# The first 60 microseconds of a fused attention and feed-forward block: early loads, products of zeros, and projections pulled in one at a time

## The chip, the core and the metric

The kernel runs on one core of one Trainium2 chip. The metric is the device time of one execution in microseconds (us). Engines: TensorE (PE; its weight loads are PEld), VectorE (DVE), ScalarE (ACT), GpSimd (POOL) and SyncE (SP). SP and POOL issue the transfers.

## The reference

A pre-norm layer on x of 2 x 1024 x 512 (float32), cut to what matters here:

```python
x = x + attention(layernorm(x), w_q, w_k, w_v, w_o)   # 32 heads of 16
x = x + ffn(layernorm(x), w_gate, w_up, w_down)       # ternary weights, quantised tokens, I = 1376
# attention: softmax(q k^T / sqrt(16)) v, all 1024 keys for each query
```

## The kernel before

**Tiling.** The heads are taken in four groups `g` of eight, and each group in two steps `s` of four heads; the queries of a batch `b` in two halves `h` of 512. That gives 32 steps `(b, h, g, s)`, in the order batch, half, group, step. A step has eight tiles `i` of 128 keys. Queries and keys are used as a high and a low part (`hi`, `lo`), each a tile of type fp32r.

**The main loop** runs over turns `T`. In a turn, `scores` makes the products of one key tile `i` of one step for the exponentials (`exp_mm`, `pse`, L558, then ACT's exp, L562) and the products for the row maxima of the next step (`max_mm`, `psm`, L518, then DVE's `max_reduce`, L528); `weigh_values` (`pso`, L588) multiplies exponentials with values. Maxima of step n are made in turns 8n to 8n + 7; the exponentials begin ten turns after (`LE = 10`), so in turns 0 to 9 there are only maxima. `max_rows` (`psn`, L541, copied to `mrow`) turns a step's maxima into a row.

**Fillers.** Between these products a planner (class `Fillers`) puts pieces of other work, written as generators: projections of keys, queries and values (`project_qk`, `psk` and `psq`, L419; `project_v`, `psv`, L459), normalisation and transposes of tokens (`norm_inputs`: statistics L353, centring L362, transposes `psx` L370, copies `xnT` L371), later the output projection and the feed-forward part. A filler says `take` when it needs a PSUM tile, `give` when it is done with it, `gap` to sleep for some turns and `pe` for what TensorE time it used. Each turn grants a budget: `pace` spreads the remaining work over the remaining turns, between 960 and 1800 ns a turn. Everything is emitted in this order; each engine works its own instructions in order.

**Round trips.** Projected keys, queries and values go to device memory (`kD`, L444; `qD`, L441; `vD`, L473 on POOL's queue) and come back rearranged: `load_k` (`kst`, L492), `load_q` (`qst`, two tiles, L500), `load_v` (L506). `lo` is made by DVE (L428) where the filler is `fast`; otherwise ACT copies (L431) and POOL makes `hi` and `lo` (L432, L433). All other transfers of the start are on SP's queue: tokens (L348), projection weights (`proj_weights`, L401).

**The start.** By hand: four tiles of tokens, weights of keys and queries of group 0; normalise the first half, project its keys and queries, load them back, normalise the second half (whose tokens use the same four buffers), project its keys, load the rest and step 1. Then the loop. Five turns before a step begins its keys and queries must exist:

```python
if (T + 5) % NT == 0 and 1 < (T + 5) // NT < NSTEP:      # NT = 8
    n = (T + 5) // NT
    b, h, g, s = steps[n]
    fill.ensure(f"k_{b}_{g}_0", f"k_{b}_{g}_1", f"q_{b}_{g}_{h}")
```

`ensure` runs the planner with an unlimited budget (`self.run(1e9)`) until the named fillers are done, so every other filler that is ready runs along. In turn 11 it asks for group 1 (step 2): after turn 10's products TensorE's order has the second half of `psv` of group 1 for the first tokens, `psk` of group 1 for the second half, `psv` of group 1 for the second half, and `psk` of group 2.

**Sums of the feed-forward weights** (`weight_sums`: POOL's transfers L680, ACT L696) start when the values of group 0 are projected; their quantisation (POOL L733, DVE L735) follows.

Of the kernel before, what the change touches and what calls it, by code (L numbers as in the profile page):

```python
# [30 lines left out]
class Fillers:  # L31
# [43 lines left out]
    def _step(self, task):  # L75

        task["begun"] = True
        if task["take"]:
            task["take"] = False
            task["kind"] = self.kind = self._bank()  # L80
            self.held.append((task["kind"], None))
        try:
            what = next(task["gen"])
        except StopIteration:
            self.tasks[task["list"]].remove(task)
            self.done.add(task["name"])
            return 0.0
        if what[0] == "pe":
            task["cost"] = max(task["cost"] - what[1], 0.0)
            return what[1]  # L90
        if what[0] == "gap":
            task["wake"] = self.now + what[1]
        elif what[0] == "take":
            task["take"] = True
            task["short"] = len(what) > 1
        else:
            task["short"] = False
            self.held.remove((task["kind"], None))
            self.held.append((task["kind"], self.now + 1))
        return 0.0  # L100

    def _candidates(self):
# [49 lines left out]
    def ensure(self, *names):  # L152

        start = self.now
        while not set(names) <= self.done:
            self.run(1e9)
            assert self.now - start < 400, names


# [57 lines left out]
def kernel(  # L217
# [39 lines left out]
    SCALE = 0.25  # L257
    LEAD = 2

    const = ctx.enter_context(tc.tile_pool(name="const", bufs=1))  # L260
    sb = ctx.enter_context(tc.tile_pool(name="sb", bufs=1))
    sp = ctx.enter_context(tc.tile_pool(name="sp", bufs=3))
# [79 lines left out]
    def norm_inputs(b, half, fast, need=()):  # L342

        tiles = range(4 * half, 4 * half + 4)
        xs = {}
        for t in tiles:
            xs[t] = sb.tile([P, H], F32, tag="x", name=f"x_{b}_{t}", bufs=4)
            nc.sync.dma_start(xs[t], x[b, t * P : (t + 1) * P, :])  # L348
        yield ("gap", 4)
        mv = sp.tile([P, 4, 2], F32, tag="mv1", name=f"mv1_{b}_{half}")  # L350
        for i, t in enumerate(tiles):
            st = sp.tile([P, 6], F32, tag="bn", name=f"bn1_{b}_{t}")
            nc.vector.bn_stats(st, xs[t])  # L353
# [7 lines left out]
        for i, t in enumerate(tiles):  # L361
            nc.vector.tensor_scalar(  # L362
                xs[t], xs[t], mv[:, i, 0:1], r[:, i : i + 1], ALU.subtract, ALU.mult
            )
            if not fast:
                yield ("gap", 1)
            yield ("take",)
            ps = spare(f"psx_{b}_{t}")
            for c in range(KC):
                nc.tensor.transpose(ps[:, c * P : (c + 1) * P], xs[t][:, c * P : (c + 1) * P], ident)  # L370
            nc.scalar.copy(  # L371
                xnT[b, half][:, :, i * P : (i + 1) * P], ps.rearrange("p (c t) -> p c t", c=KC)
            )
            yield ("give",)
            yield ("pe", 700.0)
# [20 lines left out]
        while not set(names) <= fill.done:  # L396
            yield ("gap", 1)

    def proj_weights(ap, g, name):
        w = sb.tile([P, KC, P], F32, tag="w", name=name, bufs=4)  # L400
        nc.sync.dma_start(  # L401
            w, ap.rearrange("(c p) e -> p c e", p=P)[:, :, g * P : (g + 1) * P]
        )
        return w

    def project_qk(b, g, which, h, have, fast=False):
        if which == 1 and h == 1:
            w = wt.pop((b, g))
        else:
            w = proj_weights((wqT, wkT)[which], g, f"w{'qk'[which]}_{b}_{g}_{h}")  # L410
            if which == 1:
                wt[b, g] = w
            yield ("gap", 4)
        yield from done(have)
        yield ("take",)
        name = f"{'qk'[which]}_{b}_{g}_{h}"
        ps = spare(f"ps{name}")
        for c in range(KC):
            nc.tensor.matmul(  # L419
                ps, w[:, c, :], xnT[b, h][:, c, :], start=(c == 0), stop=(c == KC - 1)  # L420
            )
            if c < KC - 1:
                yield ("pe", 860.0)
        hi = sb.tile([P, QB], F32R, tag="hi", name=f"hi_{name}", bufs=2)
        lo = sb.tile([P, QB], F32R, tag="lo", name=f"lo_{name}", bufs=2)
        if fast:
            nc.scalar.copy(hi, ps)
            nc.vector.tensor_tensor(lo, ps, hi.bitcast(F32), ALU.subtract)  # L428
        else:
            full = sb.tile([P, QB], F32, tag="full", name=f"full_{name}", bufs=1)  # L430
            nc.scalar.copy(full, ps)  # L431
            nc.gpsimd.tensor_copy(hi, full)  # L432
            nc.gpsimd.tensor_tensor(lo, full, hi.bitcast(F32), ALU.subtract)  # L433
        yield ("give",)
        yield ("pe", 860.0)
        yield ("gap", 3)
        for l, part in enumerate((hi, lo)):
            if which == 0:
                dst = qD[b, g, h][l].rearrange("(e a d) q -> a e d q", a=2, d=16)
                for a in range(2):  # L440
                    nc.sync.dma_start(dst[a], part.bitcast(F32))  # L441
            else:
                dst = kD[b, g].rearrange("(e l d) q -> l e d q", l=2, d=16)[l]
                nc.sync.dma_start(dst[:, :, h * QB : (h + 1) * QB], part.bitcast(F32))  # L444
            yield ("gap", 1)

    def step_k(n):
        b, _, g, s = steps[n]
        return kD[b, g].rearrange("(r s e) q -> s r e q", r=4, s=2)[s]

    def project_v(b, g, half, have):
        w = proj_weights(wvT, g, f"wv_{b}_{g}_{half}")
        yield ("gap", 4)
        yield from done(have)
        yield ("take",)
        ps = spare(f"psv_{b}_{g}_{half}")
# [28 lines left out]
    kst, qst, vt = {}, {}, {}  # L485
    pm, mrow, probs = {}, {}, {}

    def load_k(n, halves=((0, S),)):
        if halves[0][0] == 0:
            kst[n] = sb.tile([P, S], F32R, tag="kst", name=f"kst_{n}", bufs=3)  # L490
        for first, end in halves:
            nc.sync.dma_start(kst[n][:, first:end].bitcast(F32), step_k(n)[:, :, first:end])  # L492

    def load_q(n):
        b, h, g, s = steps[n]
# [672 lines left out]
    def now(gen):  # L1168
        for _ in gen:
            pass  # L1170
# [1 line left out]

    firsts = [norm_inputs(0, half, True) for half in range(2)]
    next(firsts[0])
    keys = [project_qk(0, 0, 1, half, [], True) for half in range(2)]
    queries = project_qk(0, 0, 0, 0, [], True)
    next(keys[0])
    next(queries)
    next(firsts[1])
    early = [project_v(0, 0, half, [f"ln_0_{half}"]) for half in range(2)]  # L1180
    next(early[0])
    for k, ap in enumerate((s_gate, s_up, s_down)):
        t = const.tile([P, 1], F32, name=f"scale{k}")
        nc.sync.dma_start(t, ap.partition_broadcast(P))
        s_sb.append(t)
    next(early[1])
    fill.kind = "s"
    now(firsts[0])
    now(keys[0])
    now(queries)  # L1190
    load_k(0, ((0, QB),))
    load_q(0)
    now(firsts[1])
    now(keys[1])
    load_k(0, ((QB, S),))
    load_k(1)
    load_q(1)
    fill.kind = "o"
    fill.done |= {"ln_0_0", "ln_0_1", "k_0_0_0", "k_0_0_1", "q_0_0_0"}

    def due_k(n):

        return NT * n - 5

    def due_v(n):
        return NT * n + 8
# [2 lines left out]
    for n, (b, h, g, s) in enumerate(steps):  # L1209
        if s == 0:  # L1210
            first_step[b, h, g] = n

    for half in range(2):
        fill.add(f"v_0_0_{half}", early[half], due=due_v(0), cost=3760.0)

    for b in range(B):
        if b:
# [11 lines left out]
        for g in range(NG):  # L1229
            n = first_step[b, 0, g]  # L1230
            if b or g:
                fill.add(f"k_{b}_{g}_0", project_qk(b, g, 1, 0, have[:1]), due=due_k(n), cost=3440.0)
                fill.add(f"k_{b}_{g}_1", project_qk(b, g, 1, 1, have), [f"k_{b}_{g}_0"], due=due_k(n), cost=3440.0)
                fill.add(f"q_{b}_{g}_0", project_qk(b, g, 0, 0, have[:1]), due=due_k(n), cost=3440.0)
                for half in range(2):
                    fill.add(f"v_{b}_{g}_{half}", project_v(b, g, half, [have[half]]), due=due_v(n), cost=3760.0)
# [45 lines left out]
    for T in range(LE + NT * NSTEP + 1):  # L1282
# [4 lines left out]

        fill.scores = int(T < LE - 1 or T >= NT * NSTEP)

        if (T + 5) % NT == 0 and 1 < (T + 5) // NT < NSTEP:  # L1290
            n = (T + 5) // NT
# [87 lines left out]
```

## Time and profile before

| | us |
|---|---|
| median of 3 runs | 1255.51 (1252.96 to 1260.84) |
| profiled execution | 1261.95, of which the span is 1259.9 |
| PE busy | 1174.2 (93%) |
| DVE busy | 854.6 (68%) |
| ACT busy | 690.2 (55%) |
| POOL busy | 251.4 (20%) |
| transfers | 136.88 MB, mean 109 GB/s |

The profiled execution is one more execution than the runs of the median, and its own time is its span and 2.05 us around it. A share of busy time is a mean over the whole span; the stages differ, so the stage tables (busy time by engine between two points of the span, with the clock granted to TensorE as a share of its full one) say more.

### The profile page before, as it was taken

Reading aid. Unit: us, or ns where it says so; the run is one execution under the profiler, and the core shown is the slowest. Engines: PE = TensorE matmul, PEld = TensorE weight load, DVE = VectorE, ACT = ScalarE, POOL = GpSimd, SP = SyncE. Lnnn points to the kernel's source line nnn. Section 1 sums busy time; section 2 is a strip of 40 time slices with the busy share of each in tenths; the row PEclk is TensorE's granted clock in tenths of the full one; section 3 lists DMA queues with packets and bytes.
Section 4 is the critical chain, followed back from the end, with each engine's and each line's share of the span. In section 5 each row is a group of like instructions: output and inputs, shape, how many; then the busy total and the mean of one; then the engine's idle time right before and its main releaser. Section 6 shows DMA issues by size and latency. Waiting matters only on the chain.

```text
span 1259.9 us, 21791 instructions
## 1 busy us (share of the span) xinstructions
PE 1174.2 (93%) x8898; PEld 526.7 (42%) x8898; DVE 854.6 (68%) x1181; ACT 690.2 (55%) x873; POOL 251.4 (20%) x286
## 2 busy tenths in 40 slices
PE   4657999999899999999999999999999998999996
PEld 2424443544345444444444444534444433344343
DVE  5431659788766667778876665576887678877173
ACT  1113855566455555666655555556666555566654
POOL 0122335556310100222001001112201011121020
PEclk9877999999999999999999999999999999999998
DMA  4446674656531432232323624233335233242200
GB/s 139 127 128 198 189 262 130 205 136 200 186 121 62 130 114 74 80 92 71 95 70 96 130 96 142 89 102 112 87 63 87 69 104 64 67 75 49 63 9 33
DMA packets 97887, 136.88 MB, mean 109 GB/s; under 512 B 33572, under 2 KB 54052, under 8 KB 97788
## 3 DMA queue, kind: packets, MB, share of 16 engines
q1 hardware_dynamic: 89916, 110.20, 30.6%
q0 software_dynamic: 7872, 25.30, 6.3%
q8 instruction: 69, 1.13, 0.4%
q14 instruction: 30, 0.25, 0.1%
HBM read 91.34 MB, written 38.24 MB: 103 GB/s over the span
## 4 chain that ended last, share of the span: by engine, by line
PE 75%; DVE 11%; issue 6%; DMA 4%; ACT 2%; POOL 1%; SPq 1%; POOLq 0%; DVEq 0%; ACTq 0%
PE pse L558 23%; PE pso L588 17%; PE psm L518 8%; PE psq L419 4%; PE psk L419 4%; DVE pm L528 4%; PE psv L459 4%; PE psy L770 4%; PE py L917 2%; PE pu L851 2%; PE pg L851 2%; PE psn L541 1%; DMA x<-in_x 1%; DMA qD<-hi_q 1%; PE psx L370 1%
## 5 line engine op out<-in xcount | busy, mean ns | idle before, releaser
L528 DVE TENSOR_REDUCE pm<-psm 128x2 f32<-128x1024 f32 x512 | 621.5, 1221 | 304.9 <-PE pse L558 192.7
L562 ACT ACTIVATE e<-pse 128x1024 f32<-128x1024 f32 x512 | 522.7, 1023 | 423.3 <-PE pse L558 316.8
L518 PE MATMUL psm<-kst,qst 32*128 32x512 f32 x2048 | 370.1, 445 | 8.0 <-ACT e L562 4.6
L558 PE MATMUL pse<-qst,kst 32*128 32x512 f32 x2048 | 370.5, 444 | 6.2 <-DVE pm L528 5.3
L558 PEld LDWEIGHTS pse<-qst,kst 32*128 32x128 f32 x2048 | 150.5, 184 | 344.3 <-issue 193.2
L588 PE MATMUL pso<-e,v 128*32 128x512 f32 x2048 | 274.5, 606 | 0.5 <-ACT po L597 0.4
L558 PE MATMUL pse<-mrow,onesr 2*128 2x512 f32 x1024 | 205.1, 398 | 0.0
L518 PEld LDWEIGHTS psm<-kst,qst 32*128 32x128 f32 x2048 | 151.0, 184 | 25.6 <-ACT e L562 13.0
L419 PE MATMUL psk<-xnT,wk 128*128 128x512 f32 x128 | 78.7, 733 | 23.3 <-DMA wk<-in_wkT 16.1
L558 PEld LDWEIGHTS pse<-mrow,onesr 2*128 2x128 f32 x1024 | 95.0, 184 | 3.4 <-ACT mrow L545 0.2
L865 POOL TENSOR_TENSOR g<-g 128x460 f32<-128x460 f32 (+1 forms) x36 | 34.2, 950 | 274.0 <-ACT g L861 274.0
L588 PEld LDWEIGHTS pso<-e,v 128*32 128x32 f32 x2048 | 40.5, 108 | 96.4 <-issue 93.5
L459 PE MATMUL psv<-wv,xnT 128*128 128x128 f32 x512 | 70.8, 289 | 2.8 <-ACT full_q L431 2.0
L459 PEld LDWEIGHTS psv<-wv,xnT 128*128 128x128 f32 x512 | 62.5, 197 | 17.3 <-issue 12.7
L419 PE MATMUL psq<-xnT,wq 128*128 128x512 f32 x128 | 66.5, 626 | 0.0
L473 POOL DMA_DIRECT2D vD<-vst x32 | 18.0, 565 | 210.6 <-ACT vst L471 210.6
L733 POOL TENSOR_SCALAR low<-raws,whalf 128x512 bf16<-128x512 f32 (+2 forms) x35 | 52.8, 1509 | 21.0 <-DVE wd L735 7.0
L770 PE MATMUL psy<-wo,OT 128*128 128x512 f32 x96 | 51.0, 639 | 2.3 <-DVE inter L873 1.8
L419 PEld LDWEIGHTS psk<-xnT,wk 128*128 128x128 f32 x128 | 25.5, 227 | 54.2 <-issue 45.4
L432 POOL CAST hi_q<-full_q 128x512 fp32r<-128x512 f32 x15 | 9.3, 619 | 152.6 <-ACT full_q L431 149.4
L851 PEld LDWEIGHTS <-xqT 128*128 128x128 bf16 x288 | 22.4, 98 | 37.6 <-issue 23.3
L826 POOL TENSOR_SCALAR xn<-x,mv,a 128x512 f32<-128x512 f32 x12 | 25.1, 2090 | 56.7 <-DVE a L803 56.6
(209 smaller groups left out, 872.3 us busy)
## 6 DMA issues: line engine op xcount, KB each, us to landing
qst<-qD SPq DMA_DIRECT2D x64, 256.0 KB
v<-vD SPq DMA_DIRECT2D x32, 512.0 KB
kst<-kD SPq DMA_DIRECT2D x31, 512.0 KB
qD<-hi_q SPq DMA_DIRECT2D x32, 256.0 KB
qD<-lo_q SPq DMA_DIRECT2D x32, 256.0 KB
vD<-vst POOLq DMA_DIRECT2D x32, 256.0 KB, 5.6
x<-in_x SPq DMA_DIRECT2D x20, 256.0 KB
wq<-in_wqT SPq DMA_DIRECT2D x16, 256.0 KB
```

The lines of the kernel that those rows point to most:

```text
L419: nc.tensor.matmul(ps, w[:, c, :], xnT[b, h][:, c, :], start=(c == 0), stop=(c == KC - 1))
L459: nc.tensor.matmul(ps[:, i * P : (i + 1) * P], xnT[b, half][:, c, i * P : (i + 1) * P], w[:, c, :], start=(c == 0), stop=(c == KC - 1),)
L518: nc.tensor.matmul(ps[:, r % 2, :], qst[n][l][rows, t * P : (t + 1) * P], kst[n][rows, kh * QB : (kh + 1) * QB], start=(l == 0), stop=(l = ...
L528: nc.vector.tensor_reduce(pm[n][:, t, kh, 2 * j : 2 * j + 2], ps, AX.X, ALU.max, negate=True)
L558: nc.tensor.matmul(ps[:, r % 2, :], left, right, start=(l == 0), stop=(l == 2))
L562: nc.scalar.activation(e, ps, AF.Exp, scale=SCALE)
L588: nc.tensor.matmul(acc[n][32 * r : 32 * r + 32, :], vt[n][:, i, r, :], e[r // 2][:, r % 2, :], start=(i == 0), stop=(i == NT - 1),)
L733: nc.gpsimd.tensor_scalar(low, w, h[:rows, m, 1:2], None, ALU.is_lt)
L770: nc.tensor.matmul(ps, OT[b, h, g][:, i * P : (i + 1) * P], wo[g], start=(g == 0), stop=(g == NG - 1),)
L851: nc.tensor.matmul(ps, xT[:, c, :], w[:, c, n : n + size], start=(c == 0), stop=(c == KC - 1))
L865: nc.gpsimd.tensor_tensor(g2[j], g2[j], g2[j], ALU.mult)
L917: nc.tensor.matmul(py, iqT[:rows, c, :], wd[:rows, c, :], start=(c == 0), stop=(c == FC - 1))
```

## The change

- The tokens of both halves are fetched at once (own buffers, tag `x2`, for the second half), with the weights of keys and queries of group 0, all on SP's queue. The value weights of group 0 and all three weights of group 1 are fetched at the start on POOL's queue (`early_weights`); `proj_weights` hands them out later without a transfer, so a value weight is fetched once for both halves.
- 24 products of the ones with a tile that is still zero run on TensorE ahead of the first transposes (`WARM`).
- The second half's statistics and centring are emitted after the first keys' products and ahead of the first queries' (for DVE: after `lo` of the keys, ahead of `lo` of the queries). The second of the two transfers of each part of the first queries, and the first load of keys, go out on POOL's queue.
- `ensure` steps only the named fillers, and others only where they hold a PSUM tile. Step 2's keys and queries are asked for three turns ahead instead of five.
- Projections of group 1 of the first batch are `fast` (ACT and DVE make `hi` and `lo`). The values of group 0 are an ordinary filler like the rest.

In TensorE's order after the change, turn 10 is followed by one product of `psk` of group 1; `psq` of group 1 stands in turns 11 and 12, `psv` of group 1 in turns 13 to 18, `psk` of group 2 in turns 19 to 23. From turn 236 to the end both orders have the same fillers in the same turns.

```diff
         while not set(names) <= self.done:
-            self.run(1e9)
+            self._back()
+            for task in self._candidates():
+                if task["name"] in names:
+                    task["wake"] = min(task["wake"], self.now)
+            ready = [t for t in self._candidates() if self._ready(t)]
+            wanted = [t for t in ready if t["name"] in names] or [t for t in ready if t["kind"]]
+            if wanted:
+                self._step(wanted[0])
+            else:
+                self.now += 1
...
+    WARM = 24
...
-            xs[t] = sb.tile([P, H], F32, tag="x", name=f"x_{b}_{t}", bufs=4)
+            if fast and half:
+                xs[t] = sb.tile([P, H], F32, tag="x2", name=f"x_{b}_{t}", bufs=6)
+            else:
+                xs[t] = sb.tile([P, H], F32, tag="x", name=f"x_{b}_{t}", bufs=4)
...
+        if fast:
+            for i, t in enumerate(tiles):
+                centre(i, t)
         for i, t in enumerate(tiles):
             if not fast:
+                centre(i, t)
                 yield ("gap", 1)
...
+    def early_weights(kind, g, tag, queue):
+        name = f"w{kind}_first_{g}"
+        if tag == "w":
+            w = sb.tile([P, KC, P], F32, tag=tag, name=name, bufs=4)
+        else:
+            w = sb.tile([P, QB], F32, tag=tag, name=name, bufs=5).rearrange("p (c e) -> p c e", c=KC)
+        queue.dma_start(w, columns(kind, g))
+        early[kind, g] = [w, 2 if kind == "v" else 1]
...
-                for a in range(2):
-                    nc.sync.dma_start(dst[a], part.bitcast(F32))
+                for a, queue in enumerate((nc.sync, nc.gpsimd if first else nc.sync)):
+                    queue.dma_start(dst[a], part.bitcast(F32))
...
     next(firsts[0])
-    keys = [project_qk(0, 0, 1, half, [], True) for half in range(2)]
-    queries = project_qk(0, 0, 0, 0, [], True)
-    next(keys[0])
-    next(queries)
+    early_weights("k", 0, "w", nc.sync)
     next(firsts[1])
-    early = [project_v(0, 0, half, [f"ln_0_{half}"]) for half in range(2)]
-    next(early[0])
+    early_weights("q", 0, "w", nc.sync)
+    for kind, g, tag in (("v", 0, "w"), ("k", 1, "w"), ("q", 1, "OT"), ("v", 1, "OT")):
+        early_weights(kind, g, tag, nc.gpsimd)
...
+    ps = scores_psum("warm")
+    for k in range(WARM):
+        nc.tensor.matmul(
+            ps[:, k % 2, :], onesr, mcols[0].rearrange("p t c -> p (t c)"), start=True, stop=True
+        )
     fill.kind = "s"
     now(firsts[0])
+    fill.done |= {"ln_0_0", "ln_0_1", "k_0_0_0", "k_0_0_1", "q_0_0_0"}
+    keys = [project_qk(0, 0, 1, half, [], True) for half in range(2)]
+    queries = project_qk(0, 0, 0, 0, [], True, True)
...
+    upto(keys[0], "give")
+    upto(firsts[1], "take")
     now(keys[0])
+    upto(queries, "give")
     now(queries)
-    load_k(0, ((0, QB),))
+    load_k(0, 0, QB, nc.gpsimd)
     load_q(0)
     now(firsts[1])
     now(keys[1])
...
-        return NT * n - 5
+        return NT * n - (3 if n == 2 else 5)
...
-                fill.add(f"k_{b}_{g}_0", project_qk(b, g, 1, 0, have[:1]), due=due_k(n), cost=3440.0)
+                fast = not b and g == 1
+                fill.add(f"k_{b}_{g}_0", project_qk(b, g, 1, 0, have[:1], fast), due=due_k(n), cost=3440.0)
```

More of the change, by code (lines that the diff above doesn't have):

```diff
@@ L97, in _step @@
             task["short"] = False
-            self.held.remove((task["kind"], None))
-            self.held.append((task["kind"], self.now + 1))
+            task["kind"], kind = "", task["kind"]
+            self.held.remove((kind, None))
+            self.held.append((kind, self.now + 1))
         return 0.0
@@ L360, in norm_inputs, with centre @@
         xnT[b, half] = sb.tile([P, KC, QB], F32, tag=f"xnT{half}", name=f"xnT{b}_{half}")
-        for i, t in enumerate(tiles):
+        def centre(i, t):
             nc.vector.tensor_scalar(
@@ L364, in norm_inputs @@
             )
+        if fast:
+            for i, t in enumerate(tiles):
+                centre(i, t)
+        for i, t in enumerate(tiles):
             if not fast:
+                centre(i, t)
                 yield ("gap", 1)
@@ L397, in done, with columns, proj_weights, project_qk @@
             yield ("gap", 1)
-    def proj_weights(ap, g, name):
-        w = sb.tile([P, KC, P], F32, tag="w", name=name, bufs=4)
[L401 to L406, printed above, removed]
+    weights = {"q": wqT, "k": wkT, "v": wvT}
+    early = {}
+    def columns(kind, g):
+        return weights[kind].rearrange("(c p) e -> p c e", p=P)[:, :, g * P : (g + 1) * P]
+    def early_weights(kind, g, tag, queue):
[6 more added lines that the diff above has]
+        early[kind, g] = [w, 2 if kind == "v" else 1]
+    def proj_weights(kind, b, g, name):
+        if early.get((kind, g), (0, 0))[1]:
+            early[kind, g][1] -= 1
+            return early[kind, g][0], False
+        w = sb.tile([P, KC, P], F32, tag="w", name=name, bufs=4)
+        nc.sync.dma_start(w, columns(kind, g))
+        return w, True
+    def project_qk(b, g, which, h, have, fast=False, first=False):
         if which == 1 and h == 1:
+            while (b, g) not in wt:
+                yield ("gap", 1)
             w = wt.pop((b, g))
         else:
-            w = proj_weights((wqT, wkT)[which], g, f"w{'qk'[which]}_{b}_{g}_{h}")
+            w, wait = proj_weights("qk"[which], b, g, f"w{'qk'[which]}_{b}_{g}_{h}")
             if which == 1:
                 wt[b, g] = w
-            yield ("gap", 4)
+            if wait:
+                yield ("gap", 4)
         yield from done(have)
@@ L451, in project_v @@
     def project_v(b, g, half, have):
-        w = proj_weights(wvT, g, f"wv_{b}_{g}_{half}")
-        yield ("gap", 4)
+        w, wait = proj_weights("v", b, g, f"wv_{b}_{g}_{half}")
+        if wait:
+            yield ("gap", 4)
         yield from done(have)
@@ L486, with load_k @@
     pm, mrow, probs = {}, {}, {}
-    def load_k(n, halves=((0, S),)):
-        if halves[0][0] == 0:
+    def load_k(n, first=0, end=S, queue=nc.sync):
+        if first == 0:
             kst[n] = sb.tile([P, S], F32R, tag="kst", name=f"kst_{n}", bufs=3)
-        for first, end in halves:
-            nc.sync.dma_start(kst[n][:, first:end].bitcast(F32), step_k(n)[:, :, first:end])
+        queue.dma_start(kst[n][:, first:end].bitcast(F32), step_k(n)[:, :, first:end])
     def load_q(n):
@@ L1185, with upto @@
         s_sb.append(t)
-    next(early[1])
+    ps = scores_psum("warm")
[3 more added lines that the diff above has]
+        )
     fill.kind = "s"
     now(firsts[0])
+    fill.done |= {"ln_0_0", "ln_0_1", "k_0_0_0", "k_0_0_1", "q_0_0_0"}
+    keys = [project_qk(0, 0, 1, half, [], True) for half in range(2)]
+    queries = project_qk(0, 0, 0, 0, [], True, True)
+    def upto(gen, what):
+        for step in gen:
+            if step[0] == what:
+                break
+    upto(keys[0], "give")
+    upto(firsts[1], "take")
     now(keys[0])
+    upto(queries, "give")
     now(queries)
-    load_k(0, ((0, QB),))
+    load_k(0, 0, QB, nc.gpsimd)
     load_q(0)
@@ L1194 @@
     now(keys[1])
-    load_k(0, ((QB, S),))
+    load_k(0, QB, S)
     load_k(1)
@@ L1198 @@
     fill.kind = "o"
-    fill.done |= {"ln_0_0", "ln_0_1", "k_0_0_0", "k_0_0_1", "q_0_0_0"}
     def due_k(n):
-        return NT * n - 5
+        return NT * n - (3 if n == 2 else 5)
     def due_v(n):
@@ L1211 @@
             first_step[b, h, g] = n
-    for half in range(2):
-        fill.add(f"v_0_0_{half}", early[half], due=due_v(0), cost=3760.0)
     for b in range(B):
@@ L1231 @@
             if b or g:
-                fill.add(f"k_{b}_{g}_0", project_qk(b, g, 1, 0, have[:1]), due=due_k(n), cost=3440.0)
[L1233 to L1236, printed above, removed]
+                fast = not b and g == 1
+                fill.add(f"k_{b}_{g}_0", project_qk(b, g, 1, 0, have[:1], fast), due=due_k(n), cost=3440.0)
+                fill.add(f"k_{b}_{g}_1", project_qk(b, g, 1, 1, have, fast), due=due_k(n), cost=3440.0)
+                fill.add(f"q_{b}_{g}_0", project_qk(b, g, 0, 0, have[:1], fast), due=due_k(n), cost=3440.0)
+            for half in range(2):
+                fill.add(f"v_{b}_{g}_{half}", project_v(b, g, half, [have[half]]), due=due_v(n), cost=3760.0)
             fill.add(f"q_{b}_{g}_1", project_qk(b, g, 0, 1, have), due=due_k(first_step[b, 1, g]), cost=3440.0)
@@ L1288 @@
         fill.scores = int(T < LE - 1 or T >= NT * NSTEP)
-        if (T + 5) % NT == 0 and 1 < (T + 5) // NT < NSTEP:
-            n = (T + 5) // NT
+        n = (T + 5) // NT
+        if 1 < n < NSTEP and T == due_k(n):
             b, h, g, s = steps[n]
```

## The prediction

> **What bounds the kernel now.** I read four views, in this order. First the busy time by stage, with the stages cut where the timeline changes its character (after the microseconds: busy time and instructions of PE, PEld, DVE, ACT, POOL, then the granted TensorE clock, the DMA share and GB/s).
>
> ```profile
> 0.00:42.46 42.46, 22.50 (x56) 12.68 (x56) 17.96 (x65) 7.13 (x11) 2.13 (x10) 0.84 0.43 130
> 42.46:60.00 17.54, 11.82 (x105) 9.21 (x104) 12.19 (x11) 1.88 (x5) 3.18 (x9) 1.00 0.39 119
> 60.00:120.00 60.00, 36.73 (x156) 20.41 (x157) 14.62 (x15) 14.79 (x40) 16.59 (x27) 0.71 0.56 173
> 120.00:160.00 40.00, 39.29 (x293) 16.84 (x292) 21.36 (x20) 29.87 (x56) 14.68 (x23) 0.97 0.59 181
> 160.00:220.00 60.00, 55.31 (x442) 26.15 (x442) 44.99 (x69) 31.84 (x40) 26.69 (x30) 0.97 0.59 193
> 220.00:320.00 100.00, 99.69 (x805) 45.58 (x800) 82.93 (x97) 58.07 (x67) 58.65 (x59) 1.00 0.62 187
> ```
>
> From 120 us on TensorE is busy 92 to 100% of these stages: there only TensorE work taken out or put in counts. Before that it stands still for 20.0 + 5.7 + 23.3 = 49 of 120 us, and in the third stage what it does runs at a granted clock of 0.71. All that this change can win lies in those 120 us. Next, TensorE's waits in the first 160 us (total, times, longest):
>
> ```profile
> PE psx L370 <- DVE x L362: 18.6, 2, 10.9
> PE psk L419 <- DMA wk<-in_wkT: 16.1, 1, 16.1
> PE psk L419 <- ACT vst L471: 5.8, 2, 5.1
> PE psm L518 <- DMA kst<-kD: 3.0, 1, 3.0
> ```
>
> Then the timeline (start, duration, engine, line, operation, count, idle time before it) for the places of these waits:
>
> ```profile
> 15.22 6.22 PE L419 MATMUL psk<-xnT,wk 128*128 128x512 f32 x8 [0.67 <-ACT xnT L371]
> 21.28 3.60 PE L419 MATMUL psq<-xnT,wq 128*128 128x512 f32 x8
> ...
> 26.13 0.69 DVE L353 BATCH_NORM_STATS2 bn<-x 128x6 f32<-128x512 f32 x1
> ...
> 32.61 3.65 PE L370 MATMUL psx<-identr,x 128*128 128x128 f32 x16 [7.74 <-DVE x L362]
> ...
> 43.80 9.36 DVE L528 TENSOR_REDUCE pm<-psm 128x2 f32<-128x1024 f32 x8
> ...
> 73.46 2.05 PE L419 MATMUL psk<-xnT,wk 128*128 128x512 f32 x2 [16.08 <-DMA wk<-in_wkT]
> ```
>
> The reader sees: the second half of the tokens is normalised only after the first queries (26.13); one projection of a warm TensorE takes 3.6 us, a cold one 6.22; and at 57 us everything stops for 16 us because the keys' weights of group 1 were asked for only at 51.7 us. Last, where the loop asks for group 1 (turn 11), the unbroken block of four projections that `ensure` pulls in:
>
> ```profile
> 108.03 3.84 PE L459 MATMUL psv<-wv,xnT 128*128 128x128 f32 x32 [0.73 <-ACT full_k L431]
> ...
> 116.97 6.54 PE L419 MATMUL psk<-xnT,wk 128*128 128x512 f32 x8 [5.10 <-ACT vst L471]
> ...
> 123.44 0.50 PE L558 MATMUL pse<-qst,kst 32*128 32x512 f32 x2
> ```
>
> No scores are made from 97 to 123.44, where turn 11 begins. I use the start of turn 11 as the milestone.
>
> **Part 1: start to first score product (42.47 before).** The 24 zero products wait for the ones (DVE, done at 3.4) and one memset: from 3.5 us. They are of the type of the scores, whose 512 columns take 0.21 us warm (pse, 0.21 in the chain of waits) and so 0.43 cold, as psk's products took 0.85 each until 20.4 us, 5 us after psk began, and 0.43 afterwards. So 12 cold (5.1 us) and 12 warm (2.6): they end at 11.2. x_0 is centred at 10.27 + 0.54 = 10.8 before; the last of the four tiles shared the transfers with two weights then, and now with POOL's four as well: 0 to 1.5 us later, I take 0.5. So 11.3, and the products cost nothing; without that cover (cold throughout: 24 x 0.43 = 10.3, end 13.8) they cost 2.5. Transposes: four per tile took 0.85 cold, ACT's copy 0.58; warm (0.43) the copies abut: first copy at 12.0, four of them, psk at 14.5 (15.22 before). psk 3.45 instead of 6.22: 17.95; psq 3.6: 21.5. lo_k at 18.6 to 19.3, and behind it on DVE the second half's block, which took 26.13 to 33.83 = 7.7: now 19.3 to 27.0, beside psq. But lo_q is queued behind it on DVE: 27.0 to 27.75 (25.53 to 26.22 before): a later first query. Its two writes go out on SP and POOL at once; writes of this kind landed 4.6 (kD, 43.91 to 48.55) to 8 us (qD, 26.8 to 34.8) after issue: I take 5.5, so 33.3; the read back is between 3 and 6.8 us (kst): 4.5, with the issue 38.4. The first-half keys' load, on POOL behind the wait for lo_q, is out at 28.5 and landed by 35. Meanwhile x_4 is centred at 25.6 (31.91 + 0.54 - 26.13 = 6.3 us into that block), second transposes and copies 4.3 (TensorE idle 4 us; taken as cold again, as after the 7.7 us at 32.61), psk 5.6 as before: TensorE is done at 35.6 and then waits 2.8 us for the query, a wait that was covered before. First score product 38.4: **4 us won**.
>
> The row first: clocks rose 5 us after psk's start though transposes ran from 10.87. The Trainium skill ("TensorE: Matmul & The Clock Gate", Part 4: PE-mode transpose) says why, that transposes do not count as busy for the gate, and Part 1 that an idle window of some 3.4 us throttles again. This speaks against the change, since 3.3 us of transposes lie between the zero products and psk; if the clock drops there, psk keeps 6.2 us and the estimate ends 2.8 us later. The sum uses the warm case, for only 3.3 us pass and the clock held over the 2 to 3 us pauses at 52 to 55 us (1.00 in that stage).
>
> **Part 2: turns 0 to 10 (first exps at 93.2 before).** Without exps a turn is two row maxima: eight took 9.36, so 2.34 a turn, with 2.05 us of value products fitting beside. Second-half keys: lo_k at 37.0, write 4.64, read 6.8: 48.5; the fifth tile is wanted at 39.1 + 9.4 = 48.5, so at most 1 us late instead of 3.0. The 16.1 us wait is gone: wk_first_1 and the others are asked for at 3 to 5 us and wanted at 50. Twelve transfers of 0.26 MB at the start are 3.1 MB; at 233 GB/s (moved from 4 to 8 us) 13.5 us, over by 14.3, before psq wants wq at 18. Step 1's keys and queries go out behind the second half at 42.5, 1 MB, wanted at 58. Turn 10 begins 20 maxima after 39.1: 24.0, plus lo_k 0.7 and the column maxima 0.7: 64.5; psn, mrow and a quarter projection 0.5: 65. Turn 11 four us later (123.44 to 127.4 is such a turn), **69 instead of 123.4: 54.4 won**, the 4 of part 1 included.
>
> **Part 3: what is put off.** The instruction orders agree again from turn 236 on, so nothing is dropped. At turn 11, psq_1_0 (3.6), two psv (3.84 each) and psk_2_0 (3.45) are still owed: **14.7 us back**, spread over later turns where TensorE is the bound; 0 in a turn that DVE sets anyway, so 10 to 14.7, I take all.
>
> **Part 4: new waits.** Queries of step 2 now end in turn 12 and are wanted in turn 16, four turns of 3.9 = 15.6 us: copy and difference 1.5, write 5.5, read 5 with its keys ahead: 13, fits. With the slowest landings in the profile (12.0 and 9.2) 23, late by 7. Groups 2 and 3 end six turns ahead (25 us; full, POOL's 1.9, 21: late by 0 to 2). I take **3 us**, ends 0 and 12. In steps 2 of group 1 ACT and DVE split the projections in place of ACT and POOL, three DVE operations of 0.69 in turns that TensorE sets: 0.
>
> **Sum:** 54.4 - 14.7 - 3 = 36.7. The profiled execution took 1261.95 (span 1259.9, 2.05 around it), 6.4 above the median of the runs, so 1225.2 on its scale and 1255.5 - 36.7 = **1218.8** on the median's.
>
> The Trainium skill ("DMA: Bandwidth & Descriptors", Issuing engines are not separate DMA queues) says that issuing from two queues only saves issue time, since all share 16 engines. The 233 GB/s row agrees that they were already 0.83 busy; by this rule the first tokens are 1.5 us later, not 0.5, and the sum 35.7.
>
> **Rivals.** (a) *The operands decide, not the weights.* For: all go to memory and back, landings of 12.0 and 9.2 us exist at 162 to 184. Then first score 42, turn 11 at 75 and 12 us of new waits: 123.4 - 75 - 14.7 - 12 = 21.7, **1233.8**. Against: the DMA share at the start is 0.43. (b) *Zeros do not lift the clock:* the products end at 13.8, psk at 18.1 and cold, everything 6.3 later: **1225.1**. No row shows zero products. (c) *More:* the clock stays up through the second transposes (psk 2.2 less), the read back takes 3, nothing is late at step 2, and DVE's turns hide 4 of the debt: 36.7 + 2 + 3 + 4 = 45.7, **1209.8**. (d) *Slower.* Put-off projections meet the quantisation of the weights on DVE, turns 27 to 100. DVE is 83% busy at 220 to 320; a statistic that waits there for its tokens (one landing took 9.2) holds the maxima behind it. It decides if the 73 turns lose over 0.5 us each (36.7 / 73); at 0.7, 51 us: **1270**. Against: only 0.31 us of 100 are idle there, and DVE's work per turn does not grow. (e) *It does not do it:* another block as at 97 to 123 is pulled in a turn later. The order shows one to three pieces per turn, so only waits could restore it: **1253**.
>
> **How the numbers follow.** Forecast 0.60 (own range 1211 to 1228), a 0.17, b 0.06, c 0.10, d 0.04, e 0.03. Faster by over 1% (about what this measurement can tell from no change): 0.60 + 0.17 + 0.06 + 0.10 = 0.93; same 0.03; slower 0.04. The range 1205 to 1239 takes in a and c with their ends (12 us of new waits, 10 of debt); outside stay d, e and tails.
>
> **What would show it.** Right: the clock full at psk's first pass; bn of the second half at 19; lo_q after 27; first psm at 38; no wait for wk in turns 5 to 9; first exps at 65; turn 11 at 69; psq_1_0 in turns 11 and 12. Wrong: psm waiting on qst in turn 16 for over 5 us; a first exp after 75; TensorE under 95% busy from 160 us on.

## The result: slower by 0.8%, and the profile after

The changed kernel takes 1266.36 us (1264.07 to 1268.15, 6 runs) against 1257.97 us (1252.96 to 1262.12, 6 runs) for the kernel before: a ratio of 1.0077, 95% interval 1.0052 to 1.0103. The forecast was 1218.8 us, faster by 36.7; it is 8.4 slower. By the prediction's own bound of 1% that is no change, to which it gave 0.03; it gave 0.93 to faster. Its profiled execution took 1268.15 us, with a span of 1266.0 (6.1 more than before).

The stages, with the same bounds and columns as before:

```profile
0.00:42.46 42.46, 26.15 (x89) 16.37 (x90) 18.99 (x67) 7.43 (x12) 7.25 (x17) 0.88 0.52 154
42.46:60.00 17.54, 17.25 (x116) 12.28 (x116) 14.63 (x13) 1.39 (x4) 3.57 (x10) 0.89 0.33 122
60.00:120.00 60.00, 44.10 (x289) 21.72 (x291) 28.14 (x31) 27.92 (x58) 12.16 (x23) 0.84 0.59 182
120.00:160.00 40.00, 39.16 (x295) 17.08 (x292) 22.12 (x24) 29.83 (x56) 11.25 (x18) 0.98 0.65 198
160.00:220.00 60.00, 54.40 (x412) 26.46 (x412) 36.67 (x44) 28.40 (x34) 25.44 (x29) 0.89 0.49 155
220.00:320.00 100.00, 89.99 (x668) 40.87 (x668) 66.81 (x81) 46.15 (x53) 50.92 (x53) 0.91 0.49 152
```

The first 120 us hold more of TensorE's work, as was forecast: 87.5 us in place of 71. But the last two stages, which TensorE filled before (55.31 of 60, 99.69 of 100, clock 0.97 and 1.00), now have gaps and a clock of 0.89 and 0.91. So there are new waits after the start, where the prediction put 3 us. TensorE's waits over the whole span (total, times, longest) name them:

```profile
PE psm L561 <- DMA qst<-qD: 24.6, 6, 12.5
PE pse L601 <- DVE pm L571: 9.9, 8, 2.9
PE psn L584 <- DVE pm L571: 7.6, 8, 2.7
PE psm L561 <- DMA kst<-kD: 5.3, 1, 5.3
```

The weights' wait (`wk`, 16.1) is gone, and a wait for the queries that come back from device memory (`qst`), which stands nowhere among TensorE's waits of before, is the largest. Now the timeline of the start (start, duration, what, count, idle time before it):

```profile
3.84 8.04 PE L1230 MATMUL warm<-mcols,onesr 128*128 128x512 f32 x24 [3.84 <-DVE lowrow L297]
11.72 1.93 PE L392 MATMUL psx<-identr,x 128*128 128x128 f32 x16
14.46 3.70 PE L462 MATMUL psk<-xnT,wk_first 128*128 128x512 f32 x8 [0.81 <-ACT xnT L393]
...
25.82 3.62 PE L392 MATMUL psx<-identr,x 128*128 128x128 f32 x16 [4.23 <-DVE x L378]
30.11 3.70 PE L462 MATMUL psk<-xnT,wk_first 128*128 128x512 f32 x8 [0.68 <-ACT xnT L393]
39.06 0.80 PE L561 MATMUL psm<-kst,qst 32*128 32x512 f32 x4 [5.25 <-DMA kst<-kD]
41.36 0.80 PE L561 MATMUL psm<-kst,qst 32*128 32x512 f32 x4 [1.50 <-DMA qst<-qD]
```

Up to the second keys this is Part 1 of the prediction to within 1 us (and they run at 3.70 where 5.6 was taken), but the operands are there at 39.06 (keys) and 41.36 (queries), where the prediction had 35 and 38.4. Then turns 9 to 16:

```profile
68.28 0.66 PE L584 MATMUL psn<-identr,mcols 128*128 128x128 f32 x4 [0.40 <-DVE pm L571]
...
73.61 0.50 PE L601 MATMUL pse<-qst,kst 32*128 32x512 f32 x2
...
74.50 1.07 PE L631 MATMUL pso<-e,v 128*32 128x512 f32 x8
...
81.98 1.12 PE L462 MATMUL psq<-xnT,wq_first 128*128 128x512 f32 x2
...
109.32 0.79 PE L561 MATMUL psm<-kst,qst 32*128 32x512 f32 x2 [12.53 <-DMA qst<-qD]
...
111.81 0.80 PE L561 MATMUL psm<-kst,qst 32*128 32x512 f32 x2 [1.69 <-DMA qst<-qD]
112.54 1.94 PE L631 MATMUL pso<-e,v 128*32 128x512 f32 x8
```

Turn 11 begins at 73.61 (it is the turn with the first `pso` group, 74.50 here and 124.34 before), 49.8 us ahead of before's 123.44. The queries of step 2 (group 1) leave TensorE at 83.1, and it stands still for them for 14.2 us in turn 16. The same happens twice more, at the first maxima of groups 2 and 3:

```profile
192.57 0.79 PE L561 MATMUL psm<-kst,qst 32*128 32x512 f32 x2 [2.52 <-DMA qst<-qD]
269.08 0.79 PE L561 MATMUL psm<-kst,qst 32*128 32x512 f32 x2 [4.63 <-DMA qst<-qD]
271.58 0.80 PE L561 MATMUL psm<-kst,qst 32*128 32x512 f32 x2 [1.71 <-DMA qst<-qD]
```

And after each stop the products run at half speed (the `pso` group above: 1.94 us where 1.07 is usual). Three stretches behind turn 16 show for how long:

```profile
109.30:114.00 4.70, 2.98 (x14) 0.80 (x14) 1.23 (x1) 1.50 (x3) 0.54 (x1) 0.50 0.31 88
114.00:118.00 4.00, 4.00 (x23) 2.86 (x20) 1.22 (x1) 1.63 (x3) 0.00 (x0) 0.50 0.06 24
118.00:122.00 4.00, 4.00 (x27) 2.48 (x25) 0.57 (x1) 0.62 (x1) 0.54 (x1) 0.58 0.22 66
```

The granted clock stays at 0.5 for some 11 us after the operands have come. Busy time times the clock that is missing gives the price: 2.98 x 0.5 + 4 x 0.5 + 4 x 0.42 = 5.2 us; in the same way 5.0 us after turn 32 (192.5 to 204) and 4.4 after turn 48 (271.5 to 283).

The account: 49.8 won at turn 11; less 14.7 put off; less 23.1 standing for `qst` (all of the 24.6 but the 1.5 at 41.36); less 14.6 at the low clock; less 2.4 more for `pm` (17.5 here, 15.1 before). That is 5.0 us slower by the sum, 6.1 by the spans. The sum leaves out that before, too, had a lower clock behind 120 us (0.97 in two stages, some 3 us by the same reckoning), so about 4 us stay open.

A count turn by turn needs no prices. From the start of each turn's first exponential (ACT, L562 before and L605 here) the lead over before is 49.8 us in turn 11 and 48.3 in turn 15. Of this 20.5 are lost from turn 15 to 17, 9.0 from 31 to 34 and 14.3 from 47 to 51: 44 of the 56 us lost in all lie around the three stops. The lead is 5.5 at turn 58 and 3.1 at turn 100, and -6.2 from turn 240 to the end. These last 12 us go bit by bit; put-off work is a likely cause, but no run shows it.

### The profile page after: what moved, and what is told of

Same layout as the page of the kernel before. It is cut to its first block, busy times and chain, and to the rows that moved or that the text cites. A ratio compares the mean times of both kernels' runs of the same rounds, so it can differ in the third digit from the quotient of the medians.

```text
span 1266.0 us, 21827 instructions
## 1 busy us (share of the span) xinstructions
PE 1184.6 (94%) x8922; PEld 533.1 (42%) x8922; DVE 855.0 (68%) x1184; ACT 689.4 (54%) x873; POOL 250.7 (20%) x287
## 4 chain that ended last, share of the span: by engine, by line
PE 71%; issue 9%; DVE 8%; DMA 6%; ACT 3%; POOL 2%; POOLq 0%; SPq 0%; ACTq 0%; DVEq 0%
PE pse L601 23%; PE pso L631 16%; PE psm L561 7%; PE psv L503 4%; PE psy L813 4%; PE psq L462 4%; PE psk L462 3%; DVE pm L571 3%; PE pu L894 2%; PE py L960 2%; PE pg L894 2%; DMA dD<-po 1%; PE psn L584 1%; ACT e L605 1%; DVE gm L934 1%
## 5 line engine op out<-in xcount | busy, mean ns | idle before, releaser
L605 ACT ACTIVATE e<-pse 128x1024 f32<-128x1024 f32 x512 | 522.6, 1023 | 462.8 <-PE pse L601 358.9
L561 PE MATMUL psm<-kst,qst 32*128 32x512 f32 x2048 | 377.8, 451 | 37.0 <-DMA qst<-qD 24.6
L631 PE MATMUL pso<-e,v 128*32 128x512 f32 x2048 | 279.5, 617 | 0.5 <-ACT po L640 0.4
L561 PEld LDWEIGHTS psm<-kst,qst 32*128 32x128 f32 x2048 | 154.1, 186 | 58.5 <-issue 26.9
L462 PE MATMUL psq<-xnT,wq 128*128 128x512 f32 x112 | 58.2, 626 | 0.0
L503 PE MATMUL psv<-wv,xnT 128*128 128x128 f32 x384 | 54.3, 291 | 0.0
L503 PEld LDWEIGHTS psv<-wv,xnT 128*128 128x128 f32 x384 | 47.3, 197 | 12.2 <-issue 11.5
L462 PE MATMUL psk<-xnT,wk 128*128 128x512 f32 x96 | 50.1, 627 | 0.0
L894 PE MATMUL pg<-wg,xqT 128*128 128x460 fp8e4 (+1 forms) x144 | 34.7, 365 | 0.0
L894 PE MATMUL pu<-wu,xqT 128*128 128x460 fp8e4 (+1 forms) x144 | 34.0, 360 | 0.0
```

The lines of the kernel that those rows point to most:

```text
L462: nc.tensor.matmul(ps, w[:, c, :], xnT[b, h][:, c, :], start=(c == 0), stop=(c == KC - 1))
L503: nc.tensor.matmul(ps[:, i * P : (i + 1) * P], xnT[b, half][:, c, i * P : (i + 1) * P], w[:, c, :], start=(c == 0), stop=(c == KC - 1),)
L561: nc.tensor.matmul(ps[:, r % 2, :], qst[n][l][rows, t * P : (t + 1) * P], kst[n][rows, kh * QB : (kh + 1) * QB], start=(l == 0), stop=(l = ...
L605: nc.scalar.activation(e, ps, AF.Exp, scale=SCALE)
L631: nc.tensor.matmul(acc[n][32 * r : 32 * r + 32, :], vt[n][:, i, r, :], e[r // 2][:, r % 2, :], start=(i == 0), stop=(i == NT - 1),)
L894: nc.tensor.matmul(ps, xT[:, c, :], w[:, c, n : n + size], start=(c == 0), stop=(c == KC - 1))
```

## Why the reads are late: the SP queue and the share of the DMA engines

The way of step 2's queries, in the timeline of SP's queue:

```profile
84.23 1.20 SPq L484 DMA_DIRECT2D qD<-hi_q  x2
85.53 1.45 SPq L484 DMA_DIRECT2D qD<-lo_q  x2
87.09 0.56 SPq L535 DMA_DIRECT2D kst<-kD  x1
91.57 4.96 SPq L543 DMA_DIRECT2D qst<-qD  x2
```

1.1 us from the last product to the first write, 2.8 of issuing, 9.5 until the writes have landed and the second read goes out (96.5), and 12.8 to 15.3 until the reads have landed: 26 to 29 us, where the prediction had 13. Other transfers run beside the reads at first (a share of 0.61 and 195 GB/s as a mean from 97 to 109.3). Towards the end, while TensorE stands there and nearly nothing else runs, the DMA engines move this (last two columns: share of 16 engines, GB/s):

```profile
106.00:109.30 3.30, 0.00 (x0) 0.01 (x1) 0.00 (x0) 0.00 (x0) 0.00 (x0) 0.50 0.26 104
```

A quarter, as much as four of 16 engines. A step's operands are 1 MB (512 KB of keys, two times 256 KB of queries), 10 us at 104 GB/s. These reads gather four blocks of 32 rows (`"(r s e) q -> s r e q"`, r = 4). The theory (N below is its rival): the slowest dimension of a transfer (the outermost count of its access pattern) sets how many engines share it, here four. The Trainium skill ("DMA: Bandwidth & Descriptors", Why a DMA increments its semaphore by 16 and not by 1) states such a rule: the engines are the largest number up to 16 that divides the slowest dimension of both patterns.

The kernel before had the sign already, in two stretches in which such reads were under way (alone in the second, beside a write of values in the first); the prediction had looked at the stage's mean of 0.39 to 0.43 and read it as room:

```profile
53.00:57.00 4.00, 1.45 (x15) 1.11 (x16) 0.83 (x2) 0.00 (x0) 0.00 (x0) 1.00 0.25 96
34.80:42.40 7.60, 6.92 (x15) 3.29 (x13) 0.00 (x0) 1.54 (x3) 0.00 (x0) 0.61 0.23 91
```

## The experiments

**1. The piecewise `ensure` undone, all else as after.**

```diff
-            self._back()
...
-                self.now += 1
+            self.run(1e9)
```

> The changed kernel, but `ensure` again runs the planner with an unlimited budget, so that turn 13 (where step 2's keys and queries are asked for) pulls in the values of group 1, the keys and the first queries of group 2 as one block (some 18 us of products). Theory L (late operands): the changed start wins 48 us up to turn 11, and this is lost in the waits for the queries and keys of steps 2, 4 and 6 (turns 16, 32, 48), which end just before they are wanted, and in the half clock after each wait. Then the block covers the way of step 2's operands through memory, groups 2 and 3 are far ahead, all three waits go, and the time is about 1228 us (1218 to 1240). Theory D (the put-off work itself costs more than its products): the order of the projections does not matter, 1260 to 1268. Theory C (the reads back are slow whatever the order): a wait of 8 us or more stays at turn 16, 1236 to 1245.

1243.6 us (1240.29 to 1244.73), against 1255.12 for the kernel before in these runs: 0.9887 (0.9837 to 0.9937). The early loads and the new order are worth 11.5 us here, and the piecewise `ensure` loses 23 of after's 1266. Theory L had 1228, 16 us less; the time lies in Theory C's range, but its sign, 8 us or more for the reads at turn 16, is not there (`qst` 2.0, `kst` 2.1 in all). The wait changed its name and stands in turn 15. TensorE's largest group of waits:

```profile
PE psm L552 <- ACT e L596: 15.1, 7, 11.5
```

In that wait of 11.5 us (117.3 to 128.85) the DMA engines were 0.85 busy at 289 GB/s: 0.65 with SP's queue (tokens, queries and values), 0.20 with POOL's. ACT stood 13.4 us for a transfer of the weight sums (`raw`), which is ahead of the exponential in its order. That is another limit, reached from the other side.

**2. The piecewise `ensure` kept, with a larger budget ahead of turn 48**, so that the groups' projections come earlier by themselves.

```diff
         share = min(max(fill.pace([w[4:] for w in ffns]), SHARE), MORE)
+        if T < 48:
+            share = MORE
```

> The changed kernel with one line more: in turns 0 to 47 the budget for fillers is 1800 ns a turn. The first queries of group 1 then end in turn 9 instead of 12, those of group 2 in turn 19 instead of 26, of group 3 in turn 30 instead of 42; the products are the same. Theory L: the waits at turns 16, 32 and 48 go, and the time is 1225 to 1235 us. Theory D: nothing changes but the order of the same work, 1260 to 1268. Theory C: a wait at turn 16 of 5 us or more stays, 1235 to 1245.

1239.5 us (1238.37 to 1241.0), 0.9859 (0.9811 to 0.9908): a little above Theory L's range and in Theory C's, but without C's sign, a wait of 5 us or more for the reads in turn 16. The waits for `qst` fall from 24.6 to 3.3 (the longest 1.6), others come: 7.9 on ACT's exp at 149 (0.98 of the DMA engines busy there) and 6.3 on `v`. The wait for the first `kst` stays (5.2, after 5.3).

**3. The reads cut into four**, one for each block of 32 rows, with everything else as after.

```diff
-            rows = qD[b, g, h][l].rearrange("(r s e) q -> s r e q", r=4, s=2)[s]
-            nc.sync.dma_start(q.bitcast(F32), rows)
+            for r in range(4):
+                row = 64 * r + 32 * s
+                nc.sync.dma_start(
+                    q[32 * r : 32 * r + 32, :].bitcast(F32), qD[b, g, h][l][row : row + 32, :]
+                )
```

(`load_k` in the same way.)

> The changed kernel, but each read back of keys and queries is cut into four transfers of 32 partitions (128 in all before, gathered from four blocks of 32 rows). While TensorE waits for the queries at turns 16 and 48 the DMA share is 0.23 to 0.26 of 16 engines at 89 to 104 GB/s, as if four engines carried the reads. Theory C: with 32 rows in a transfer more engines carry it, the reads of a step (1 MB) take 4 to 5 us instead of 10, and though SP issues 12 transfers for 3 a step, the wait at turn 16 falls from 14 to 4 to 8 us and those at turns 32 and 48 go: 1240 to 1250 us. If the share of 0.25 has another reason, the 12 issues of 0.55 us only make the operands later: 1266 to 1274.

1235.18 us (1228.87 to 1235.55), 0.9812 (0.976 to 0.9865): 31 us less than after, and below the expected range, from the same bytes. `qst` waits fall from 24.6 to 7.7.

**4. The piecewise `ensure` alone, in the kernel before.**

> The kernel before, with the new `ensure` alone (only the named fillers, and those that hold a PSUM tile); start, loads and due turns are those of before. Theory L: the block at 97 to 123 us goes, which saves its cold and idle part, some 12 us, but steps 2, 4 and 6 now wait for their operands, 30 us or more with the half clock: 1270 to 1285 us, slower than before. Theory D: only the idle part of the block goes, 1243 to 1250.

1287.88 us (1282.48 to 1289.38), 1.0247 (1.0188 to 1.0307): 33 us lost, 3 more than the upper end expected. TensorE's waits have the new one, and the old one for the weights:

```profile
PE psm L528 <- DMA qst<-qD: 19.4, 6, 9.7
...
PE psk L429 <- DMA wk<-in_wkT: 15.1, 1, 15.1
```

**5. Reads cut into four and the larger budget**, runs 2 and 3 together.

> The changed kernel with both remedies: reads back cut into four transfers of 32 partitions, and a budget of 1800 ns in turns 0 to 47. Theory L with C: an earlier projection and a shorter way back add up as far as waits are left; the best case is the sum of my prediction, 1219 us, and I expect 1222 to 1232. If the waits left in both (8 to 10 us, at a DMA share of 0.8 to 0.97) come from the amount of transfers in turns 12 to 20 and not from the order, 1232 to 1240, no better than the reads alone.

**1218.5 us** (1217.14 to 1220.84), 0.9686 (0.9662 to 0.9709): faster than both kernels, and the lowest median that was run. The stage from 60 to 120 us is now nearly full, at full clock:

```profile
60.00:120.00 60.00, 57.88 (x428) 28.17 (x427) 34.91 (x36) 42.46 (x86) 19.43 (x34) 1.00 0.74 223
```

The two largest of TensorE's waits that are left:

```profile
PE pse L609 <- DVE pm L579: 7.9, 8, 2.2
PE pso L639 <- DMA v<-vD: 6.3, 1, 6.3
```

That this is the forecast's number is partly chance: the forecast knew nothing of wide reads, which help the kernel before too, as the next run shows.

**6. Reads cut into four in the kernel before.**

> The kernel before with the reads back cut into four transfers of 32 partitions, nothing else. Theory C: the wait of 16 us for wk in turn 5 is in part the queue behind the reads of step 0 and 1, so it shrinks to 5 to 12 us, and the wait for kst (3.0) goes: 1243 to 1253 us. If only just-in-time operands suffer from slow reads, no change within 0.5%: 1252 to 1262.

1240.37 us (1239.49 to 1241.01), 0.9863 (0.9843 to 0.9883): 16 us from that alone. The wait for the weights, 16.1 before:

```profile
PE psk L419 <- DMA wk<-in_wkT: 5.3, 1, 5.3
```

So the 16.1 us wait for the weights, which the change removed by asking earlier, was two thirds the slow reads ahead of them: `wk`, issued at 51.7 behind the reads of step 1, landed at 73.4. Against this kernel run 5 is 21.9 us faster (1240.37 - 1218.5); that is what the change with its waits mended is worth where the reads are wide, the larger budget included, which was not tried in the kernel before. That wide reads go over more engines shows in the stage from 42.46 to 60 us, which holds the reads of step 1: a share of 0.76 and 225 GB/s in this run, 0.39 and 119 before.

**7. The weight sums started later** (after the queries of group 1).

```diff
-    fill.add("sums", weight_sums(), ["v_0_0_1"], "back")
+    fill.add("sums", weight_sums(), ["v_0_0_1", "q_0_1_0"], "back")
```

> The changed kernel, with the sums of the feed-forward weights (one transfer of 256 KB on POOL's queue and one ACT pass a turn) started after the first queries of group 1 (turn 13) instead of after the values of group 0 (turn 6); the order of the projections is the same. Theory C in its wider form (the transfers of those turns stretch the way): the queries of step 2 no longer share the engines with six of these transfers, and ACT's copy of the queries does not stand behind a pass that waits for one (7.7 us in the changed kernel): the wait at turn 16 falls from 14 us to 2 to 7, the waits at turns 32 and 48 stay or grow, 1250 to 1260 us. If the form of the reads is all, 1263 to 1269.

1265.99 us (1262.58 to 1268.64), 1.0067 (1.0044 to 1.009): the time of after, where 6 to 16 us less had been expected; it lies in the range of the other theory, "If the form of the reads is all". TensorE's wait for `qst`:

```profile
PE psm L561 <- DMA qst<-qD: 23.2, 7, 9.6
```

The wait in turn 16 is shorter (9.6 + 1.7), but the total is the same. Starting the sums later does not mend it.

**8. Run 5 without the products of zeros** (`WARM = 0`).

> The kernel of the run with both remedies, without the 24 zero products. By the prediction the first keys' products are cold again: psk 6.2 us instead of 3.7, the transposes 3.65 instead of 1.93, so 3 to 5 us later at the first score product, and 3 to 5 us more at the end. If the milestone is set by the second half's tokens and the queries' way through memory, the loss is the same, since these follow psk on DVE. If the products of zeros did nothing, 0.

1219.61 us (1216.5 to 1230.42), 0.9714 (0.9664 to 0.9763), next to run 5's 0.9686 (0.9662 to 0.9709): no difference that these runs can tell, where 3 to 5 us were expected. The interval is too wide to exclude 3 us by the time alone, so the start has to be read. Its timeline of the start:

```profile
10.39 3.68 PE L392 MATMUL psx<-identr,x 128*128 128x128 f32 x16 [10.39 <-DVE x L378]
14.74 3.70 PE L462 MATMUL psk<-xnT,wk_first 128*128 128x512 f32 x8 [0.68 <-ACT xnT L393]
...
30.52 5.85 PE L462 MATMUL psk<-xnT,wk_first 128*128 128x512 f32 x8 [0.68 <-ACT xnT L393]
```

The first keys run at full speed (3.70) behind transposes alone, which took 6.22 before in the same place. The second keys are slow (5.85 for 3.70), but they lie beside the way of the operands: the first score product comes at 36.30, 0.9 us after run 5's (35.36).

Run 6 shows the same thing in the kernel before: its edit does not touch the start, and yet the first keys, 6.22 us before, ran there at full speed:

```profile
10.96 3.61 PE L370 MATMUL psx<-identr,x 128*128 128x128 f32 x16 [10.96 <-DVE x L362]
15.24 3.70 PE L419 MATMUL psk<-xnT,wk 128*128 128x512 f32 x8 [0.68 <-ACT xnT L371]
```

So the slow first keys, which the products of zeros were to mend, belong to one execution of that start and not to the start.

**9. The reads cut into two**, of 64 rows each: more transfers than after, each with a slowest dimension of 2.

```diff
-            nc.sync.dma_start(q.bitcast(F32), rows)
+            for r in range(0, 4, 2):
+                nc.sync.dma_start(q[32 * r : 32 * r + 64, :].bitcast(F32), rows[r : r + 2])
```

> The kernel after, with each read of kst and qst cut into two transfers of 64 partitions (slowest count 2) where e3_split_reads cut them into four of 32 partitions; everything computed as before. W (what widens a read is the count of its slowest dimension, and nothing else: four blocks go on four engines, two blocks on two): a read now keeps 2 engines busy in place of 4, so the DMA share while TensorE waits for qst falls to 0.13 to 0.2 (0.25 in the kernel after) or stays at 0.25 where two transfers fall on different engines; the wait in turn 16 grows to 15 us or more, and the time is 1270 to 1310. N (the number and the smallness of the transfers gave the gain of e3_split_reads: more of them are in flight at once): half of that gain, 1245 to 1255, with a share of about 0.5.

**1378.0 us** (1376.92 to 1378.74), 1.0979 (1.0956 to 1.1001). The two theories pointed to opposite sides, and N is out: more and smaller transfers made it 112 us slower than after. W has the sign, and its figure for the engines, though its price was 68 us too low at the upper end. TensorE's waits for `qst`:

```profile
PE psm L566 <- DMA qst<-qD: 98.4, 16, 19.3
```

A stretch of the wait that ends at 235.99 (busy times, clock, DMA share, GB/s):

```profile
229.00:235.90 6.90, 0.00 (x0) 0.00 (x0) 0.00 (x0) 0.00 (x0) 0.00 (x0) 0.50 0.13 52
```

Nothing else runs there: a share of 0.13, as much as two of 16 engines, and 52 GB/s, half of after's 0.26 and 104. The 6 waits for `qst` of after became 16.

**10. Reads cut into four with the old `ensure`.**

> The kernel after with reads cut into four transfers and with the ensure of before (an unlimited budget until the named fillers are done); its place in the set is between e1_old_ensure (1243.6: old ensure, slow reads) and e5_split_budget (1218.5: wide reads, new ensure with a larger budget ahead of turn 48). L (the new ensure costs only through the lateness of the operands, so that anything that brings them in time is as good): 1218 to 1226. O (the blocks that the old ensure pulls in cost time by themselves, as the stop of the scores at 97 to 123 us before, and the piecewise ensure is needed): 1230 to 1240, with a block of projections ahead of turn 11's scores and ACT as releaser.

1235.38 us (1233.72 to 1236.45), 0.9846 (0.9822 to 0.987): O's range. No wait for `qst` or `kst` is among its larger groups of waits; here the block costs, as before the change (timeline):

```profile
76.49 1.13 PE L453 MATMUL psq<-xnT,wq_first 128*128 128x512 f32 x2
79.50 3.84 PE L494 MATMUL psv<-wv_first,xnT 128*128 128x128 f32 x32 [1.88 <-DVE lo_q L462]
84.07 3.84 PE L494 MATMUL psv<-wv_first,xnT 128*128 128x128 f32 x32 [0.73 <-ACT vst L506]
89.83 3.70 PE L453 MATMUL psk<-xnT,wk 128*128 128x512 f32 x8 [1.92 <-ACT vst L506]
94.20 3.70 PE L453 MATMUL psk<-xnT,wk 128*128 128x512 f32 x8 [0.68 <-ACT full_k L465]
98.63 3.70 PE L453 MATMUL psq<-xnT,wq 128*128 128x512 f32 x8 [0.73 <-ACT full_k L465]
```

From 77.6 to 102.27 no scores are made, and 5.9 us of that TensorE stands still. Outside the block the waits on ACT's exponentials grew most against run 5: 10.5 us in all, 3.0 there. The runs with the new start, in a table (ratio to the kernel before in the same runs):

| `ensure` | reads on four engines | reads cut into four |
|---|---|---|
| in one block | 1243.6 (0.9887) | 1235.4 (0.9846) |
| piecewise | 1266.4 (1.0077) | 1235.2 (0.9812) |
| piecewise, larger budget early | 1239.5 (0.9859) | 1218.5 (0.9686) |

The piecewise `ensure` loses 23 us with narrow reads and next to nothing with wide ones; only with wide reads and the larger budget is there a gain, 17 us. A kernel with the block, wide reads and the larger budget was not run, so whether these 17 us are the piecewise `ensure`'s or the budget's alone is not shown.

## Why the prediction was wrong, step by step

- **The step that failed is Part 4**, new waits "3 us, ends 0 and 12". They cost 23.1 us standing and 14.6 at the low clock, 37.7. Three terms of it were mis-sized. The read back, 5 us, took 12.8 to 15.3: 1 MB goes at some 100 GB/s in this form, 10 us if nothing else runs (runs 3, 6 and 9 show that it is the form), and other transfers shared the way. The writes, 5.5, took 9.5 from the end of their issue, with 0.69 of the DMA engines busy meanwhile. And the upper bound was made of the slowest single landings of the profile (9.2 for the read), though a step reads three such transfers, 1 MB in all. It said "23, late by 7"; it was 26 to 29, late by 14.2.
- **The range failed with it**, by what it left out: the three stops, of 14.2, 4.0 and 6.3 us, were each followed by some 11 us with the clock at half. Part 1 had counted a cold clock, Part 4 had not. And the stops of groups 2 and 3 (2.5 and 6.3 us for `qst`, another 1.5 without a releaser just before the first) were put at 0 to 2.
- **Part 2** was too large by 4.6: turn 11 at 73.61, forecast 69, so 49.8 won instead of 54.4. All of it lies ahead of turn 10: the read of the first keys' half from POOL's queue took 10.4 us from issue to landing (three to 6.8 in the sum), queries came at 41.36, and the value products behind them ran at half clock (from 42.09 on, 16 products in 3.78 us where 2.05 is usual). The first products for exponentials came at 69.79, forecast 65.
- **Part 1** held: zeros from 3.84, transposes at 11.72 (forecast 11.3), keys warm at 14.46 (14.5). The second half's transposes ran at half speed, as Part 1 took (3.62 us, 1.93 for the first half's), but the keys behind them at full speed: rival c's gain came there without its condition, a clock that stays up. But the steps are right only as positions: in run 8, without the zeros, the first score comes 0.9 us later and no loss can be measured. What sets the first score is the way of the operands.
- **Part 3**, 14.7 us put off, was not measured by itself; the account above closes to 1 us with it, or to some 4 with before's own low clock.
- **The rivals.** The mechanism is the one of rival a, "The operands decide": it had the first score at 42 (41.36), turn 11 at 75 (73.6), and 12 us of waits where there were 37.7; with 37.7 in its sum it ends 4.0 us slower than before. It was set aside "Against: the DMA share at the start is 0.43", and this is the misreading: a mean of stretches with most engines at work (0.83 from 4 to 8 us) and others with as much as four (0.23 from 34.8 to 42.4). Rival b's condition did not come (the zero products took 0.43 us each up to 8.7 us and 0.23 to 0.24 after, and the first keys ran at 3.70), nor rival e's block. Rival d, the only one that ended slower, named DVE in turns 27 to 100; 44 of the 56 us lost lie around the three waits for transfers, so its sign came true by another mechanism.
- **Part 1's clock rule** (the Trainium skill, "TensorE: Matmul & The Clock Gate", Part 4: transposes do not count for the gate) fits before (keys slow behind transposes) but not runs 6 and 8 (keys fast behind transposes alone). The measurement decides: in run 8 the keys were fast 4.35 us after the transposes began, in run 6, with the start of before, 4.28. What differed from before's execution is open.
- **Slips in the sums** that did not carry the miss: the twelve transfers at the start of Part 2 are fourteen (eight of tokens, six of weights), its 20 maxima at 1.17 us are 23.4 and not 24.0, and Part 4's 1.5, 5.5 and 5 add up to 12 and not 13.

## What to carry to other kernels

Before moving a producer closer to its consumer, price the round trip by the bytes and the DMA share of a stretch in which that transfer runs alone, not by the landing time of some instance nor by a stage's mean share; a share that stays at 0.25 or 0.13 while everybody waits says that the shape of the transfer, not the load, is the limit. Cut such a transfer so that each piece's slowest dimension is large (here 32 rows). To a stop of TensorE of some microseconds in the main loop add the time at the low clock behind it: here 4 to 5 us each, for stops of 4 to 14 us.

## What was not expected of the hardware

- Cutting each read of 256 or 512 KB into four pieces of one block gave 31 us (after) and 16 us (before); cutting it into two pieces of two blocks cost 112. Share and rate in waits without other work: 0.26 and 104 GB/s with four blocks in a transfer, 0.13 and 52 with two.
- In the waits of runs 1 and 2 that other transfers filled, the DMA engines moved 289 to 316 GB/s at 0.85 to 0.98 busy.
- The zero products did lift the clock (0.43 us each up to 8.7 us, 0.23 to 0.24 after), but it was up at the first keys without them too (runs 6 and 8). In the kernel before, whose start is run 6's, it was not: one execution of a start does not tell how fast its first products are.
